# Convolution results stored as 196 pixels a quarter in column order, centering products over four rounds, raw weights two rounds later

## The chip, the cores and the metric

The kernel runs on one core of one Trainium2 chip, in float32 throughout. The metric is the time of the program on the device, in microseconds (us). The kernel before took 2997.26 us, the median of 3 runs (2994.66 to 2997.37).

TensorE (PE) multiplies matrices and writes its results to PSUM, an accumulation memory of eight banks. VectorE (DVE) and ScalarE (ACT) work elementwise on PSUM and on SBUF, the on-chip memory; GpSimd (POOL) works on SBUF. SyncE (SP) and ScalarE issue the transfers, which 16 DMA engines carry out.

## The reference

The input x is 32 images of 384 channels and 28 x 28 pixels. A ConvNeXt block with a response normalisation is followed by a gate over channels:

```python
y = conv_general_dilated(x, dw_w, (1, 1), [(3, 3), (3, 3)], feature_group_count=C) + dw_b
mu, var = mean(y, channels), mean(square(y - mu), channels)
y = (y - mu) * rsqrt(var + 1e-6) * ln_g + ln_b
y = gelu(y @ w1 + b1)                       # 384 -> 1536
gx = sqrt(sum(square(y), pixels))
y = grn_g * (y * gx / (mean(gx, features) + 1e-6)) + grn_b + y
x = x + y @ w2 + b2                         # 1536 -> 384
avg, mx, mn = mean(x, pixels), max(x, pixels), min(x, pixels)
logits = concat(avg @ W1.T, grouped(mx, W2_1) * W2_2, mn @ W3.T) @ Wfc.T
out = sigmoid(logits + x)
```

## The kernel before, in words

There are two stages.

**The convolution stage** runs 48 rounds (`NK`), of 8 channels each, over all 32 images at once. In a round, `conv` (L733) multiplies turned image rows (`xt`) with small banded matrices of the taps (`tmat`), 160 matmul instructions, into four PSUM tiles `pc`. `settle` empties them: ScalarE adds the bias and writes `ye` (L754), DVE adds the results into the running channel sum `acc` (L761), and DVE transposes blocks of 32 x 32, so that images come to lie on partitions (L767). The result `yt` holds, for each partition (a quarter of the rows of one image: 4 quarters x 32 images) and each of the 8 channels, 7 rows of 32 places, of which 28 are pixels and 4 are a gap: `YP` = 224 places for `YR` = 196 pixels. ScalarE squares the pixels (L778) and POOL adds the squares (L781). Two transfers on ScalarE's queue store `yt` to the DRAM tensor `yd` (L850). DVE also turns the image rows for the round after next (`turn_x`, L526). Two sets of four PSUM tiles alternate, so `conv` of a round waits until the round two before has been emptied.

SP loads in program order: image rows five rounds ahead (`load_x`, L466), tap tables (`load_t`, L485), and what the table `loads` sets for a round. Every instruction of this stage is held in program order on its engine. A transfer also waits, before its issue, on the signal that it takes over from a transfer about a dozen earlier.

Beside the convolution the weights are prepared. The first weight matrix is loaded in three parts (`raw1`) in rounds 5, 6 and 7. In round 9, behind the convolution's matmuls, `center_sums` does 72 matmul instructions (36 products of two instructions) with `ln_b` and `ln_g` (L640); DVE takes out the new bias and the column means `mcol`. In rounds 10, 11 and 12 `center_means` spreads the means over the partitions and `center_w` takes them out of the weights (L671). From round `U1` = 13 on, `form_w` makes the first layer's sums of weight blocks on POOL and ScalarE (L610 to L616), which SP stores to DRAM (L857) two rounds later. The second matrix is loaded by `raw2` from round `U2` - 3 on, and its 38 forms are made in rounds `U2` = 26 to `U2E` = 45.

**The image stage** runs over the 32 images; each has two products, done with fewer multiplications through sums of blocks. `load_y` loads an image's convolution results from `yd` into `yi` (L332), `normed` multiplies them by the inverse deviation `rb` (L352), POOL makes sums of rows of blocks (`forms_up`, L396), `up` does the first product (L982), ScalarE the gelu (L930) and the squares (L950), POOL sums of blocks again (`sums`, L1119), and `down` the second product (L1156) in 38 steps of 3 products. DVE adds each step's PSUM result `pz` to the quarters of the image `xt` that it belongs to (L1172; L1174 where it is the last term of a quarter, with the bias and a sum). Quarter j of an image is the rows 4k + j. `gate_store` computes the gate and stores the image. While one image goes down, gelu and squares of the next lie beside it on ScalarE; a planner sets the order of what isn't held.

Of the kernel before, what the change touches and what calls it, by code (L numbers as in the profile page):

```python
# [14 lines left out]
P = 128  # L15
C = 384
# [205 lines left out]
def convnext_gate_kernel(  # L222
# [18 lines left out]
    smp = ctx.enter_context(tc.tile_pool(name="smp", bufs=3))  # L241

    fs = [dram.tile([P + 1, FL], F32, name=f"fs_{cb}") for cb in range(CB)]
    yd = dram.tile([P, C, YP], F32, name="yd")
    rsd = dram.tile([P, YR], F32, name="rsd")
    u1d = dram.tile([KT, P, NS, P], F32, name="u1d")
    u2d = dram.tile([ND // UD, P, UD * KD * P], F32, name="u2d")
# [53 lines left out]
    EARLY_G = (0, 1)  # L301

    def load_y(b):
        yi = yis[b] = yip.tile([P, CB, NQD, YP], F32, tag="yi", name=f"yi_{b}")

        with tc.issue_after(last_u2[-1]) if last_u2 else ExitStack():
            for cb in range(CB):
                ins = load_y_part(b, yi, cb, 0, P)
                if b == 1:
                    tc.keep_in_program_order(ins)  # L310
        if b > 1:
            load_rb(b)
# [21 lines left out]
            yd.rearrange("(q b) c n -> b c q n", b=B)[b, cb * P + p0 : cb * P + p1],  # L334
        )

    def rows(v):

        return v.rearrange("p q (k w) -> p (q k) w", w=PW)[:, :, :HW]

    def flat(v):

        return v.rearrange("p q n -> p (q n)")

    def normed(b, cbs=range(CB)):

        if b not in accs:
            accs[b] = (
                xp.tile([P, CB, NT], F32, tag="x", name=f"acc_{b}") if b == 1 else room_acc
            )  # L350
        for cb in cbs:
            ins = nc.vector.tensor_tensor(  # L352
                accs[b][:, cb].rearrange("p (k w) -> p k w", w=HW),
                rows(yis[b][:, cb]),
                rbs[b].rearrange("p q (k w) -> p (q k) w", w=HW),
                ALU.mult,
            )
            if b <= 2:
                tc.keep_in_program_order(ins)
# [40 lines left out]
    with ExitStack() as one:  # L400
# [13 lines left out]
            return pscs[(n_now + other) % 2].tile([P, 512], F32, tag="pc", name=name)  # L414


        scr = yip.tile([P, CB, NQD, YP], F32, tag="yi", name="scr")
        scr = scr.rearrange("p k q n -> p (k q n)")
        nscr = 0

# [129 lines left out]
        w1r = ws.rearrange("p (k f) -> p k f", f=FF)  # L550
        w1v = ws.rearrange("p (k t m c) -> p t k m c", t=KT, m=3, c=P)
        w2v = ws.rearrange("p (t k m c) -> p t k m c", t=KD, k=4, c=P)
        U1, U2, U2E = 13, 26, NK - 3
        stores = []
        SG = 24

# [83 lines left out]
                nc.tensor.matmul(dst, w, v, start=False, stop=True, skip_group_check=True)  # L640
            )

        def center_sums(pb):

            for n in range(FB):
                for cb in range(CB):
                    end_product(
                        pb[:, 2 * n : 2 * n + 2], w1r[:, cb, n * P : (n + 1) * P], lr[:, cb]
                    )
# [55 lines left out]
        for n, f, *args in (  # L705
            (0, load_x, 2, (0, 1)), (0, load_x, 2, (1, 2)),
            (1, load_t, 1), (3, vectors),
            (2, load_x, 3, (0, 1)), (2, load_x, 3, (1, 2)),
            (3, load_x, 4, (0, 1)), (3, load_x, 4, (1, 2)),
            (13, gate_rows), (14, load, wfc[: 3 * R], wfcT), (15, load, w22b, w22.broadcast_to([P, R])),  # L710
            (4, load_t, 2), *((5 + i, raw1, i) for i in range(CB)),
            *((k - 5, load_x, k // XR, (k % XR, k % XR + 1)) for k in range(5 * XR, NK)),
            *(
                (TR * m - 6 + q, load_t, m, None, (q,))
                for m in range(3, NK // TR)
                for q in range(NQD)
            ),
            *((U2 - 3 + i, raw2, i) for i in range(3)),
        ):
            loads[n].append((f, args))  # L720
# [21 lines left out]
        def settle(n, pcs, yt):  # L742

            ye = yep.tile([P, NQD, 2, NN], F32, tag="ye", name=f"ye_{n}")
            last = n == NK - 1
            for q in range(NQD):
                for g in range(2):
                    c = TC * n + 2 * q + g
                    dst, src = ye[:, q, g, :], pcs[q][:, g * NN : (g + 1) * NN]
                    if last and q >= 2:  # L750
                        keep(nc.vector.tensor_scalar(dst, src, dwb[:, c : c + 1], None, ALU.add))
                    else:
                        keep(
                            nc.scalar.activation(  # L754
                                dst, src, AF.Identity, bias=dwb[:, c : c + 1], scale=1.0
                            )
                        )
            def sums():

                for q in range(NQD):  # L760
                    keep(nc.vector.tensor_tensor(acc, acc, pcs[q][:, : 2 * NN], ALU.add))  # L761

            if not last:
                sums()
            for h in range(2):
                keep(
                    nc.vector.transpose(  # L767
                        yt[:, 2 * h : 2 * h + 2].rearrange("p q g (k w) -> p (q g k) w", w=PW),
                        ye[:, 2 * h : 2 * h + 2].rearrange("p q g (k b) -> p (q g k) b", b=PW),
                    )  # L770
                )
            yv = yt.rearrange("p q g (k w) -> p (q g k) w", w=PW)[:, :, :HW]
            if last:
                sums()
            if n >= NK - 2:
                direct(n, yt)
            sq = sqp.tile([P, TC * YR], F32, tag="sq", name=f"sq_{n}")
            keep(nc.scalar.activation(sq.rearrange("p (k w) -> p k w", w=HW), yv, AF.Square))  # L778
            for h in range(2):
                keep(  # L780
                    nc.gpsimd.tensor_tensor(  # L781
                        ssum, ssum, sq[:, h * NQD * YR : (h + 1) * NQD * YR], ALU.add
                    )
                )

        def direct(n, yt):

            c0 = (TC * n) % P
            for h in range(NQD):
                keep(  # L790
                    (nc.scalar if n == NK - 1 else nc.sync).dma_start(
                        yis[0][c0 : c0 + TC, CB - 1, h, :],
                        yt[h * B : h * B + 1].rearrange("p q g n -> p (q g) n"),
                    )
                )

        def first_image(cb):

            keep(
                nc.scalar.activation(  # L800
                    room_acc[:, cb].rearrange("p (k w) -> p k w", w=HW), rows(yis[0][:, cb]),
                    AF.Identity,
                )
            )

        accs[0] = room_acc
        for n in range(NK):
# [12 lines left out]
            ends = [p[:, 2 * NN :] for p in pcs]  # L820
            if n == 6:
                end_product(ends[0][:, :NV], vrows, ident[:, :NV])
            if n == 9:
                center_sums(ends[0])
            if n == SG:
                for cb in range(CB):
                    end_product(
                        ends[cb][:, : 3 * R], wfc[:, cb * P : (cb + 1) * P],
                        ident[:, : 3 * R],
                    )  # L830
            if 10 <= n < 10 + CB:
                center_means(n - 10)
            yt = ycp.tile([P, NQD, 2, YP], F32, tag="yc", name=f"yt_{n}")
            if n + 2 < NK:
                turn_x(n + 2)
# [1 line left out]
            if n == 6:  # L837
                keep(nc.vector.tensor_copy(vecs, ends[0][:, :NV]))
                keep(nc.vector.tensor_copy(lr[:, :, 0], lnb_t))
                keep(nc.vector.tensor_scalar(lr[:, :, 1], lng_t, -1.0 / C, None, ALU.mult))  # L840
            if n == 9:
                pbv = ends[0][:, : 2 * FB].rearrange("p (f v) -> p f v", v=2)
                keep(nc.vector.tensor_tensor(b1f, pbv[:, :, 0], b1_t, ALU.add))
                keep(nc.vector.tensor_copy(mcol, pbv[:, :, 1]))
            if 10 <= n < 10 + CB:
                center_w(n - 10)
            for h in range(2):
                c0 = TC * n + NQD * h
                keep(
                    nc.scalar.dma_start(  # L850
                        yd[:, c0 : c0 + NQD, :],
                        yt[:, 2 * h : 2 * h + 2].rearrange("p q g n -> p (q g) n"),
                    )
                )
            while stores and stores[0][0] <= n:
# [2 lines left out]
            if 2 <= n < CB + 1:  # L858
                sequences(n - 1)
            if n == NK - 11:  # L860
                yis[0] = yip.tile([P, CB, NQD, YP], F32, tag="yi", name="yi_0")
# [146 lines left out]
    def finish(part):  # L1008
# [3 lines left out]
        if part == 1:  # L1012
# [7 lines left out]
            )  # L1020
            keep(
                nc.vector.tensor_scalar(
                    mu.rearrange("p (k w) -> p k w", w=HW),
                    turned.rearrange("p (k w) -> p k w", w=PW)[:, :, :HW],
                    dws, 1.0 / C, ALU.add, ALU.mult,
                )
# [49 lines left out]
    def sums(b):  # L1076

        if b not in ops:
# [7 lines left out]
            if b >= max(1, B - 2):  # L1086


                n = KD * NQ4
                if b == B - 2:  # L1090
                    more = yip.tile([P, CB, NQD, YP], F32, tag="yi", name="more")
# [40 lines left out]
    def down(b, hooks):  # L1132
# [13 lines left out]
        for i, (opnd, _, bk, reads) in enumerate(STEPS):  # L1146
# [244 lines left out]
```

## Time and profile before

| what | value |
|---|---|
| median of 3 runs | 2997.26 us |
| the profiled execution's own time | 2999.83 us |
| its span, first to last instruction | 2998.1 us |
| PE busy | 2924.5 us (98%) |
| DVE busy | 2014.6 us (67%) |
| ACT busy | 1761.2 us (59%) |
| POOL busy | 2365.0 us (79%) |
| DMA moved | 614.51 MB, mean 205 GB/s |
| store yd<-yt | 96 of 448 KB, 5.1 us to landing |
| load yi<-yd | 95 of 448 KB, 6.0 us to landing |

In the profile, L12 is line 12 of the kernel; `yt<-ye` means that the tile yt is written from ye. The page's forty slices show each engine's busy share in tenths, TensorE's granted clock and the DMA engines' share. A group's row has the count, the busy time, the mean of one instruction in ns, and the idle time of its engine just before, with what ended it. The chain is followed back from the last instruction, at each step to what released it. A busy PE is not PE at its peak, since matmuls are pipelined.

### The profile page before, as it was taken

The numbers are of one execution on the slowest core, as the hardware profiler recorded it, in microseconds if no ns is written. First come the engines' busy times: TensorE is split into PE (matmuls) and PEld (weight loads), VectorE is DVE, ScalarE is ACT, GpSimd is POOL, SyncE is SP. The second block draws the span as 40 slices with busy tenths as digits, with TensorE's granted clock in tenths as the row PEclk, the third lists the DMA queues.
The fourth block names the chain that finished last, engine by engine and source line by source line (L and its number), as shares of the span: only waits on it lengthen the run. The fifth ranks groups of instructions, "written<-read, shape, count | busy, mean of one in ns | idle before, by whom it ended". The sixth has DMA issues, their size and how long they took to land.

```text
span 2998.1 us, 53084 instructions
## 1 busy us (share of the span) xinstructions
PE 2924.5 (98%) x19156; PEld 2304.5 (77%) x19156; DVE 2014.6 (67%) x4444; ACT 1761.2 (59%) x2854; POOL 2365.0 (79%) x1768
## 2 busy tenths in 40 slices
PE   9998998899999999999999999999999999999998
PEld 8777774777777777777777777777777777777777
DVE  5677777766666666666666666666666666666665
ACT  3454565656666666666666666556666666666671
POOL 2356657888888888888888888888888888888897
PEclk9898999999999999999999999999999999999999
DMA  9789966556666666666666666666666656666545
GB/s 249 215 258 279 289 229 203 175 179 191 195 193 200 200 202 201 200 198 197 199 201 205 206 204 209 201 203 206 205 201 187 208 190 190 193 198 200 196 149 197
DMA packets 281263, 614.51 MB, mean 205 GB/s; under 512 B 26587, under 2 KB 102057, under 8 KB 281001
## 3 DMA queue, kind: packets, MB, share of 16 engines
q1 hardware_dynamic: 253154, 526.62, 57.0%
q10 hardware_dynamic: 27846, 84.49, 7.6%
q8 instruction: 154, 2.52, 0.4%
q14 instruction: 109, 0.88, 0.1%
HBM read 516.47 MB, written 94.48 MB: 204 GB/s over the span
## 4 chain that ended last, share of the span: by engine, by line
PE 83%; DMA 6%; DVE 4%; POOL 3%; issue 2%; ACT 1%; SPq 0%; ACTq 0%; DVEq 0%; POOLq 0%
PE ph_C L982 14%; PE ph_A L982 13%; PE ph_B L982 12%; PE pz_A L1156 8%; PE pz_C L1156 8%; PE pz_D L1156 7%; PE pz_F L1156 7%; PE pc L733 4%; PE pz_H L1156 2%; PE pz_I L1156 2%; PE pz_E L1156 2%; DMA yd<-yt 2%; DVE room L352 1%; PE pz_B L1156 1%; PE pz_G L1156 1%
## 5 line engine op out<-in xcount | busy, mean ns | idle before, releaser
L365 ACT ACTIVATE y<-y,vecs,gsc 128x784 f32<-128x784 f32 x375 | 359.9, 1030 | 446.3 <-DVE gsc L1064 446.3
L1119 POOL TENSOR_TENSOR d_room<-y 128x588 f32<-128x588 f32 x250 | 359.8, 1443 | 293.9 <-PE pz_B L1156 217.8
L930 ACT ACTIVATE y<-y,b1f 128x784 f32<-128x784 f32 x384 | 348.0, 945 | 221.4 <-DVE y L1001 197.3
L982 PE MATMUL ph_C<-room,ws 128*128 128x392 f32 x1224 | 456.4, 494 | 3.7 <-DVE y L999 2.4
L982 PE MATMUL ph_A<-room,ws 128*128 128x392 f32 x1220 | 454.1, 494 | 5.0 <-ACT te L991 5.0
L1119 POOL TENSOR_TENSOR d_room<-d_room,y 128x588 f32<-128x588 f32 x308 | 442.8, 1442 | 16.7
L982 PE MATMUL ph_B<-room,ws 128*128 128x392 f32 x1220 | 452.2, 493 | 1.4 <-DVE te L999 1.4
L733 PE MATMUL pc<-xt,tmat 28*128 28x224 f32 (+3 forms) x7680 | 383.7, 362 | 33.8 <-DVE stats L761 17.0
L733 PEld LDWEIGHTS pc<-xt,tmat 28*128 28x128 f32 (+2 forms) x7680 | 318.3, 173 | 97.3 <-issue 45.1
L982 PEld LDWEIGHTS ph_C<-room,ws 128*128 128x128 f32 x1224 | 230.6, 190 | 181.8 <-DVE y L999 21.3
L982 PEld LDWEIGHTS ph_A<-room,ws 128*128 128x128 f32 x1220 | 232.2, 190 | 175.5 <-ACT te L991 5.6
L982 PEld LDWEIGHTS ph_B<-room,ws 128*128 128x128 f32 x1220 | 231.7, 191 | 164.2 <-DVE te L999 2.2
L781 POOL TENSOR_TENSOR stats<-stats,sq 128x784 f32<-128x784 f32 x96 | 177.6, 1850 | 223.6 <-ACT sq L778 219.8
L950 ACT ACTIVATE stats<-y 128x784 f32<-128x784 f32 x381 | 326.8, 858 | 9.0
L1119 POOL TENSOR_TENSOR d_room<-y,d_room 128x588 f32<-128x588 f32 x214 | 306.6, 1439 | 27.0 <-PE pz_D L1156 15.9
L396 POOL TENSOR_TENSOR room<-room 128x392 f32<-128x392 f32 x298 | 298.8, 1019 | 11.6
L1119 POOL TENSOR_TENSOR y<-y 128x588 f32<-128x588 f32 x180 | 258.5, 1436 | 6.5
L997 DVE TENSOR_TENSOR y<-y,ph_B 128x392 f32<-128x392 f32 x252 | 135.5, 558 | 151.4 <-ACT y L930 123.5
L995 DVE TENSOR_TENSOR y<-y,ph_C 128x392 f32<-128x392 f32 x386 | 216.3, 562 | 27.4 <-ACT y L991 0.9
L1156 PE MATMUL pz_A<-d_room,u 128*128 128x196 f32 x1050 | 204.7, 330 | 1.8 <-DMA u<-u2d 0.8
L761 DVE TENSOR_TENSOR stats<-stats,pc 128x448 f32<-128x448 f32 x192 | 119.1, 620 | 114.8 <-ACT ye L754 96.1
L1156 PEld LDWEIGHTS pz_A<-d_room,u 128*128 128x128 f32 x1050 | 178.2, 190 | 10.8 <-POOL d_room L1119 1.8
(277 smaller groups left out, 5495.7 us busy)
## 6 DMA issues: line engine op xcount, KB each, us to landing
u<-u2d SPq DMA_DIRECT2D x487, 384.0 KB, 3.8
ws<-u1d SPq DMA_DIRECT2D x380, 320.0 KB, 3.0
ws<-u2d SPq DMA_DIRECT2D x121, 384.0 KB, 4.1
yd<-yt ACTq DMA_DIRECT2D x96, 448.0 KB, 5.1
yi<-yd SPq DMA_DIRECT2D x95, 448.0 KB, 6.0
x<-in_x SPq DMA_DIRECT2D x32, 1176.0 KB, 5.6
out<-x ACTq DMA_DIRECT2D x31, 1176.0 KB, 7.6
xi<-in_x SPq DMA_DIRECT2D x120, 196.0 KB, 6.0
```

What stands on the lines that cost most here:

```text
L365: eng.activation(out, in_, AF.Identity, bias=add, scale=mul)
L396: tc.keep_in_program_order(eng.tensor_tensor(d, o[in0], o[in1], op))
L733: nc.tensor.matmul(pcs[q][PW * j0 : PW * j1, g * NN + k0 * PW : g * NN + k1 * PW], t[PW * q : PW * q + HW, m0 : m0 + PW * (j1 - j0)], xt[P ...
L761: keep(nc.vector.tensor_tensor(acc, acc, pcs[q][:, : 2 * NN], ALU.add))
L781: nc.gpsimd.tensor_tensor(ssum, ssum, sq[:, h * NQD * YR : (h + 1) * NQD * YR], ALU.add)
L930: ins = nc.scalar.activation(y, y, AF.Gelu, bias=b1f[:, f : f + 1], scale=1.0)
L950: ins = nc.scalar.activation(stats[:, :NT], ys[b][:, f, :], AF.Square, accum_out=ssqs[b][:, f : f + 1])
L982: ins = nc.tensor.matmul(banks[t, bk][:, :NH], wts[t, g][:, gi, :], o[opnd], start=(first == 1), stop=True, skip_group_check=True,)
L995: ins = nc.vector.tensor_tensor(d, d, p, ALU.add)
L997: ins = nc.vector.tensor_tensor(d, d, p, ALU.subtract)
L1119: eng.tensor_tensor(d[0], o[a][0], o[c][0], ALU.add if sign == "+" else ALU.subtract)
L1156: nc.tensor.matmul(pz[:, :NQ4], wt[:, i % UD, t, :], o[opnd][0][:, t, :], start=(first and t == 0), stop=(t == KD - 1), skip_group_check=True,
```

## The change

The results between the stages lose their gaps. The transpose now writes each block so that pixels lie in column order: place w * 7 + k for column w and row k of a quarter, so that the 196 pixels come first and the 28 places of the four gap columns last. `yd` and `yi` hold 196 places a quarter, and the two stores a round leave the gap out. Everything between works on 196 pixels in column order; `normed` and `first_image` read without gaps. Where column order meets row order again, the pattern of one operand changes: the channel mean `mu` in `finish` is written in column order, and in `down` the PSUM result is read in steps of 7 places, against rows of the image.

The 36 centering products of round 9 are spread over rounds 10 to 13, nine in each; the means and `center_w` move from rounds 10 to 12 to rounds 12 to 14. The three loads of the first matrix move from rounds 5 to 7 to rounds 7 to 9. `U1` goes from 13 to 15 and `U2` from 26 to 28, with all that hangs on them (the forms, their stores, the three loads of the second matrix), while the end `U2E` stays.

```diff
-    yd = dram.tile([P, C, YP], F32, name="yd")
+    yd = dram.tile([P, C, YR], F32, name="yd")
...
-        yi = yis[b] = yip.tile([P, CB, NQD, YP], F32, tag="yi", name=f"yi_{b}")
+        yi = yis[b] = yip.tile([P, CB, NQD, YR], F32, tag="yi", name=f"yi_{b}")
...
             ins = nc.vector.tensor_tensor(
-                accs[b][:, cb].rearrange("p (k w) -> p k w", w=HW),
-                rows(yis[b][:, cb]),
-                rbs[b].rearrange("p q (k w) -> p (q k) w", w=HW),
+                accs[b][:, cb], flat(yis[b][:, cb]), flat(rbs[b]),
                 ALU.mult,
             )
...
-        U1, U2, U2E = 13, 26, NK - 3
+        U1, U2, U2E = 15, 28, NK - 3
...
-        def center_sums(pb):
+        NC, FC = 10, 3
 
-            for n in range(FB):
+        def center_sums(g, pb):
+
+            for n in range(g * FC, (g + 1) * FC):
                 for cb in range(CB):
                     end_product(
...
-            (4, load_t, 2), *((5 + i, raw1, i) for i in range(CB)),
+            (4, load_t, 2), *((7 + i, raw1, i) for i in range(CB)),
...
                     nc.vector.transpose(
-                        yt[:, 2 * h : 2 * h + 2].rearrange("p q g (k w) -> p (q g k) w", w=PW),
-                        ye[:, 2 * h : 2 * h + 2].rearrange("p q g (k b) -> p (q g k) b", b=PW),
+                        yt[:, 2 * h : 2 * h + 2].rearrange("p q g (w k) -> p (q g) k w", w=PW),
+                        ye[:, 2 * h : 2 * h + 2].rearrange("p q g (k b) -> p (q g) k b", b=PW),
                     )
...
-            yv = yt.rearrange("p q g (k w) -> p (q g k) w", w=PW)[:, :, :HW]
+            yv = yt.rearrange("p q g n -> p (q g) n")[:, :, :YR]
...
-            if n == 9:
-                center_sums(ends[0])
+            if NC <= n < NC + FB // FC:
+                center_sums(n - NC, ends[0])
...
-            if 10 <= n < 10 + CB:
-                center_means(n - 10)
+            if NC + 2 <= n < NC + 2 + CB:
+                center_means(n - NC - 2)
...
-            if n == 9:
-                pbv = ends[0][:, : 2 * FB].rearrange("p (f v) -> p f v", v=2)
-                keep(nc.vector.tensor_tensor(b1f, pbv[:, :, 0], b1_t, ALU.add))
-                keep(nc.vector.tensor_copy(mcol, pbv[:, :, 1]))
-            if 10 <= n < 10 + CB:
-                center_w(n - 10)
+            if NC <= n < NC + FB // FC:
+                fs_now = slice((n - NC) * FC, (n - NC + 1) * FC)
+                pbv = ends[0][:, : 2 * FB].rearrange("p (f v) -> p f v", v=2)[:, fs_now]
+                keep(nc.vector.tensor_copy(mcol[:, fs_now], pbv[:, :, 1]))
+                keep(
+                    nc.vector.tensor_tensor(b1f[:, fs_now], pbv[:, :, 0], b1_t[:, fs_now], ALU.add)
+                )
+            if NC + 2 <= n < NC + 2 + CB:
+                center_w(n - NC - 2)
...
                         yd[:, c0 : c0 + NQD, :],
-                        yt[:, 2 * h : 2 * h + 2].rearrange("p q g n -> p (q g) n"),
+                        yt[:, 2 * h : 2 * h + 2].rearrange("p q g n -> p (q g) n")[:, :, :YR],
...
-                    mu.rearrange("p (k w) -> p k w", w=HW),
+                    mu.rearrange("p (w k) -> p k w", w=HW),
...
-                pzh = pz[:, :NQ4].rearrange("p (k w) -> p k w", w=HW)
+                pzh = pz[:, :NQ4].rearrange("p (w k) -> p k w", w=HW)
```

More of the change, by code (lines that the diff above doesn't have):

```diff
@@ L335, in load_y_part @@
         )
-    def rows(v):
-        return v.rearrange("p q (k w) -> p (q k) w", w=PW)[:, :, :HW]
     def flat(v):
@@ L414, in bank1 @@
             return pscs[(n_now + other) % 2].tile([P, 512], F32, tag="pc", name=name)
-        scr = yip.tile([P, CB, NQD, YP], F32, tag="yi", name="scr")
+        scr = yip.tile([P, CB, NQD, YR], F32, tag="yi", name="scr")
         scr = scr.rearrange("p k q n -> p (k q n)")
@@ L777, in settle @@
             sq = sqp.tile([P, TC * YR], F32, tag="sq", name=f"sq_{n}")
-            keep(nc.scalar.activation(sq.rearrange("p (k w) -> p k w", w=HW), yv, AF.Square))
+            keep(nc.scalar.activation(sq.rearrange("p (c n) -> p c n", n=YR), yv, AF.Square))
             for h in range(2):
@@ L792, in direct @@
                         yis[0][c0 : c0 + TC, CB - 1, h, :],
-                        yt[h * B : h * B + 1].rearrange("p q g n -> p (q g) n"),
+                        yt[h * B : h * B + 1].rearrange("p q g n -> p (q g) n")[:, :, :YR],
                     )
@@ L800, in first_image @@
                 nc.scalar.activation(
-                    room_acc[:, cb].rearrange("p (k w) -> p k w", w=HW), rows(yis[0][:, cb]),
-                    AF.Identity,
+                    room_acc[:, cb], flat(yis[0][:, cb]), AF.Identity,
                 )
@@ L860, in convnext_gate_kernel @@
             if n == NK - 11:
-                yis[0] = yip.tile([P, CB, NQD, YP], F32, tag="yi", name="yi_0")
+                yis[0] = yip.tile([P, CB, NQD, YR], F32, tag="yi", name="yi_0")
             for cb in range(CB):
@@ L1090, in sums @@
                 if b == B - 2:
-                    more = yip.tile([P, CB, NQD, YP], F32, tag="yi", name="more")
+                    more = yip.tile([P, CB, NQD, YR], F32, tag="yi", name="more")
                     more = more.rearrange("p k q n -> p (k q n)")
```

## The prediction

> **What bounds the kernel now.** I read the page first, its busy shares and its forty slices.
>
> ```profile
> PE 2924.5 (98%) x19156; PEld 2304.5 (77%) x19156; DVE 2014.6 (67%) x4444; ACT 1761.2 (59%) x2854; POOL 2365.0 (79%) x1768
> PE   9998998899999999999999999999999999999998
> PEclk9898999999999999999999999999999999999999
> DMA  9789966556666666666666666666666656666545
> ```
>
> There are two stages. From slice 9 on (about 600 us) TensorE is full, at full clock, with DMA at 0.6. The waits of TensorE between 600 and 2850 us are only these:
>
> ```profile
> PE ph_C L982 <- DVE y L999: 2.4, 11, 0.5
> PE pz_A L1156 <- DMA u<-u2d: 0.8, 2, 0.4
> PE pz_A L1156 <- DVE x L1172: 0.7, 1, 0.7
> ```
>
> So nothing in that stage can become faster by a cheaper load or a cheaper DVE instruction: it can only become slower. The first 460 us, the convolution's 48 rounds, are different. In one window over them DMA stands at 0.85, TensorE at a granted clock of 0.89, DVE at 321.9 of 460 us. Undisturbed, 160 matmuls of a round take 7.2 us (the chain has 633 of them in 28.52 us); the 48 rounds take about 9 us each. All that this change can win lies here. The chain, in order of time, shows the one long piece that the change touches:
>
> ```profile
> 94.40 14.68 PE pc L733 x313
> 109.08 12.77 PE pc L640 x72
> 121.86 5.74 PE pc L733 x77
> ```
>
> and the stretches around it (columns: window, length, busy of PE, PEld, DVE, ACT, POOL, granted clock, DMA share, GB/s):
>
> ```profile
> 102.00:122.00 20.00, 20.00 (x268) 18.87 (x255) 7.95 (x10) 5.48 (x11) 7.38 (x4) 0.75 0.98 258
> 122.00:131.00 9.00, 9.00 (x168) 7.88 (x168) 6.64 (x10) 4.29 (x9) 1.65 (x1) 0.80 0.25 93
> 131.00:139.00 8.00, 7.90 (x169) 6.70 (x168) 6.15 (x9) 4.82 (x10) 2.04 (x2) 1.00 0.13 52
> ```
>
> While TensorE does the 72 centering products the transfers run ahead until their buffers are full, and then the DMA engines idle: 9.0 x 0.75 + 8.0 x 0.87 = 13.7 us of it.
>
> **Part 1: centering products spread, raw matrix later.** The work stays: 72 products x 178 ns = 12.8 us, now four times 3.2 us in rounds 10 to 13, and the eight mean products of three rounds (1.16 us each) two rounds later. The small DVE reads (0.13 and 0.15 us) become four pairs, +0.8 us in all on a DVE that has about 2 us a round free. What can be won is the idle DMA time: at most 13.7 us. The other bound is TensorE itself. Round 9 ends at 109.1; then four rounds of 7.2 + 3.2 us and two mean products give 153 us for the start of round 14, which now starts at 159.4. That is -6.5. With the rounds a little faster than 7.2 (the undisturbed ones of this stretch take 6.4) it is -9. I take **-8 us**. The three raw loads (768 KB each, SP queue) move from rounds 5 to 7 to rounds 7 to 9, past the image loads (four a round) and the tap-table loads of those rounds. DMA is full from 50 to 122 us, so the same bytes stall TensorE two rounds later; this I count as nothing. The cover is that round 10 needs the last one only at its end, some 10 us after its issue; were it late, the matmuls behind the centering products in TensorE's queue would wait, a few us. The second raw load, the forms and their stores move by two rounds, and 38 second-layer forms go into 17 rounds for 19. That is 12% more per round on POOL, which was busy 37.7 of 50 us at its fullest; some 2 us more in 50 fit. SP already waits 63.2 us for POOL before form stores, with image loads queued behind; I put 0 to +4 us on it and take 0, as nearly all of those waits are for forms that are stored two or three rounds after they are made.
>
> **Part 2: the packets.** A store of 448 KB in 128 packets of 3584 B becomes 392 KB in 512 packets of 784 B, since the 112 B gap now stands between quarters in SBUF. Two narrow windows price this. The first has only the two stores of one round (256 packets and 32 signals, 9 ns each by the packet records) in 4 us; the second, 3 us long, only the store of the row of statistics, 128 packets of 784 B from SBUF to DRAM, the very form that comes.
>
> ```profile
> q10 hardware_dynamic: 288, 0.92, 58.0%
> ```
> ```profile
> q1 hardware_dynamic: 144, 0.10, 10.5%
> ```
>
> 58.0% x 16 x 4 us is 37.1 us, less 0.3 for signals: 144 ns a packet. 10.5% x 16 x 3 us is 5.04 us, less 0.14: 38 ns a packet. A round's stores go from 256 x 144 = 36.9 to 1024 x 38 = 38.9 us of engine time: the 12.5% fewer bytes are eaten by the packets. Over 16 engines that is +0.12 us a round, +6 us if all 48 were bound by DMA; about 0.6 of the stage has DMA over 0.9, so **+3.6 us**. The bounds are -9 (bytes count, packets do not) and +6. The loads of it had 512 packets before (896 B); they get 7% shorter, in a stage where they are hidden.
>
> **Part 3: strides.** The transpose writes every 28 B in SBUF, and the additions of the second half read PSUM every 28 B. No row of this trace has such a stride. The nearest rows are the same instructions without it:
>
> ```profile
> L767 DVE STREAM_TRANSPOSE yt<-ye 128x896 f32<-128x896 f32 x96 | 100.7, 1087 | 1.6 <-ACT ye L754 1.6
> L1172 DVE TENSOR_TENSOR x<-x,pz_C 128x196 f32<-128x196 f32 x320 | 103.1, 355 | 78.8 <-PE pz_C L1156 78.5
> ```
>
> An element costs 1.04 ns (392 elements 558 ns, 196 elements 355). Two rules of the Trainium skill part here. "VectorE: DVE Perf Modes", section on mode 1x, says that fp32 with odd strides still makes one result a cycle: +0. "SBUF — State Buffer", section on the DMA port swizzle, says that SBUF is read in lines of 16 B and PSUM in lines of 8 B, that at least two hits a line hide the latency, and that each access to a new line pays. 28 B hit a new line every time; it gives no figure, so as an estimate from the rows I take a second cycle for each element: +0.93 us a transpose (96 of them) and +0.20 us an addition (51 an image). By the first rule parts 2 and 3 come to +3.6; by the second to +25 in each place, worked out under the rivals. I take the first, since 1.04 ns is one step of the engine and contiguous PSUM reads show no finer one, but keep the second in the range. The multiply at L352 loses its gaps (969 ns median); it lies behind a full TensorE, 0.
>
> **Sum.** 2999.8 us (the profiled execution; span 2998.1) - 8 + 3.6 = 2995.4. That execution stands 2.6 above the median 2997.3, so against the median **2993 us**, own range 2984 to 2999.
>
> **Rivals.**
> *Strided PSUM reads cost* (ends slower). The place is the end of each image's second half:
>
> ```profile
> 1528.00:1532.00 4.00, 4.00 (x26) 4.00 (x25) 2.83 (x9) 3.49 (x4) 2.22 (x3) 1.00 1.03 376
> 1532.00:1536.00 4.00, 4.00 (x15) 2.50 (x14) 3.97 (x10) 2.25 (x5) 3.84 (x4) 1.00 1.03 414
> ```
>
> (The third busy column is DVE.) DVE is at 2.83 and then 3.97 of 4 us, with reductions of 0.96 us behind the additions. Some 20 of an image's 51 additions fall in the last 14 us; 20 x 0.20 = 4 us against about 3 us of free time makes DVE some 1 us late where the next image's first results want their banks and DVE. 31 images x 0.8 us: **+25, 3018 us**. Earlier a step of TensorE is 0.99 us with at most two additions at a pitch of 0.27 us; at 0.47 they still fit. It decides from about +0.15 us an addition; at +0.3 (pitch 0.57 x 51 plus 10 us of other DVE work against 38 steps of 0.99 us) the whole half is bound by DVE, over 3035 us. For it: the 8 B line. Against: DVE sits idle before nearly every addition.
> *Strided SBUF writes cost.* A round of DVE takes 2.1 (turning images) + 2.9 (sums) + 2.1 (transposes) = 7.1 us; +1.9 makes 9.0, as long as the mean round. The rounds shorter than that would stretch by up to 1.9 us, some half of 48, less what DMA stalls hide: +25, **3018 us**.
> *The stores land later.* Each ring now holds 32 packets of a store for 8, in turn with 6 KB image packets of the SP queue. The stores' landing is 8.6% of the chain of the first 600 us, 52 us, and ScalarE waits at its store issue with the next round's eviction behind it, then DVE's sums, then TensorE two rounds on. A third longer: +17, less the gain of 8: **3006 us**. Against: image packets then pass the stores sooner, and those are on the chain as well.
> *Nothing changes*: the idle DMA time only moves to another round: **2997 us**.
>
> **How the numbers follow.** Chances: the forecast 0.40, PSUM reads 0.19, SBUF writes 0.13, later stores 0.15, nothing 0.13. A measurement here tells about 0.2%, 6 us, from no change. Of the forecast's 0.40, some 0.26 lies below 2991 and 0.13 within; with the few gains of "nothing" faster is 0.30. Within: 0.13 plus most of "nothing" plus a little of the later stores, 0.24. Slower 0.46, from the three costs. The range goes from 2984 to 3032: below lies 0.07, above (dear PSUM reads, or both strides) 0.11.
>
> **What would show it.** The group at L640 in four pieces of 3.2 us and DMA over 0.7 in the two rounds after round 9; L767 at 1087 and L1172 at 355 ns as before (right) or near 2000 and 560 (rivals one and two); queue 10 with 49,152 packets of 784 B at 38 ns; start of round 14 near 151 us. It is wrong if TensorE's waits in the second stage grow beyond 10 us, or if store landings pass 7 us.

## The result, and the profile after

The changed kernel takes **3041.6 us** (median, 3038.2 to 3043.0) against 2997.3 us (2994.7 to 2997.4): a ratio of **1.0136, 95% interval 1.0121 to 1.0151**. It is 44 us slower by these medians and 41 us by the ratio, which is used from here on; the forecast was 2993 us, with a range up to 3032.

The lines of the changed kernel's page that answer to the busy shares and slices of before:

```profile
PE 2941.0 (97%) x19156; PEld 2313.3 (76%) x19156; DVE 2082.3 (69%) x4450; ACT 1760.5 (58%) x2854; POOL 2366.2 (78%) x1768
...
PE   9987898899999999999999999999999999999998
...
PEclk9888888999999999999999999999999999999999
DMA  9879976545665666666665666656655565665545
```

DVE has 68 us more work, and TensorE's granted clock reads 8 (0.8 to 0.9) in slices 2 to 7, where before it read 8 in slices 2 and 4 alone. From slice 8 on TensorE's rows are the same as before. By the start times in the two traces:

| | before | after | difference |
|---|---|---|---|
| profiled span | 2998.1 | 3036.4 | +38.3 |
| start of round 14 | 159.4 | 154.8 | -4.6 |
| start of round 26 | 266.2 | 274.7 | +8.5 |
| end of the convolution (last matmul of `conv`) | 450.2 | 485.3 | +35.1 |
| third load of `rb` to the end (the image stage) | 2438.4 | 2439.0 | +0.6 |

So nearly the whole loss arises in the convolution stage, behind the start of round 14. The groups of the two strided instructions after the change (busy, mean ns, idle before):

```profile
L763 DVE STREAM_TRANSPOSE yt<-ye 128x896 f32<-128x896 f32 x96 | 164.8, 1795 | 1.7 <-ACT ye L750 1.7
L1170 DVE TENSOR_TENSOR x<-x,pz_C 128x196 f32<-128x196 f32 x320 | 103.1, 355 | 77.0 <-PE pz_C L1154 76.5
```

The transpose that writes SBUF every 28 B went from 1087 to 1795 ns. The addition that reads PSUM every 28 B takes 355 ns as before (the prediction shows both rows of before). `normed` (now L348) keeps its median of 968 ns (969 before). Stores and loads between the stages, first the queue's line before and then the changed kernel's lines (packets, MB, share of 16 engines; below it KB and median us to landing):

```profile
q10 hardware_dynamic: 27846, 84.49, 7.6%
```
```profile
q10 hardware_dynamic: 64710, 78.98, 8.3%
...
yd<-yt ACTq DMA_DIRECT2D x96, 392.0 KB, 6.9
yi<-yd SPq DMA_DIRECT2D x95, 392.0 KB, 5.5
```

Fewer bytes take more engine time. By the packet records of the convolution stage's stores alone it is 142.6 us of each engine for 119.3: 49,184 packets of 784 B at 46.4 ns for 12,288 of 3584 B at 155 ns.

The centering products, in the chain of waits in order of time (start, length), and the windows where the DMA engines idled before, with the next 16 us:

```profile
114.16 6.10 PE pc L729 x113
120.25 2.10 PE pc L634 x18
122.35 7.96 PE pc L729 x160
130.31 2.10 PE pc L634 x18
```
```profile
122.00:131.00 9.00, 9.00 (x171) 8.01 (x170) 8.27 (x11) 4.73 (x10) 3.70 (x2) 0.81 0.88 199
131.00:139.00 8.00, 8.00 (x130) 7.75 (x137) 6.55 (x8) 3.62 (x9) 3.69 (x2) 0.79 1.03 251
139.00:155.00 16.00, 16.00 (x273) 13.95 (x258) 11.83 (x18) 6.38 (x12) 5.38 (x3) 0.89 0.63 162
```

A piece of 18 product instructions takes 2.1 us, and DMA stands at 0.88 and 1.03 where it stood at 0.25 and 0.13. Part of the idle time has moved behind it: 0.63 from 139 to 155 us, for 0.79 before.

**A loop that the prediction did not look at.** The timelines of a calm stretch of each kernel (start, length, engine, count; in brackets the wait ahead of it), first before, then after:

```profile
167.90 2.80 ACT L754 ACTIVATE ye<-pc,dwb 128x224 f32<-128x224 f32 x8
168.70 2.89 DVE L761 TENSOR_TENSOR stats<-stats,pc 128x448 f32<-128x448 f32 x4 [1.39 <-ACT ye L754]
171.50 2.10 DVE L767 STREAM_TRANSPOSE yt<-ye 128x896 f32<-128x896 f32 x2
173.70 1.51 ACT L778 ACTIVATE sq<-yt 128x1568 f32<-128x1568 f32 x1 [3.00 <-DVE yt L767]
...
175.63 2.80 ACT L754 ACTIVATE ye<-pc,dwb 128x224 f32<-128x224 f32 x8
```
```profile
307.70 2.80 ACT L750 ACTIVATE ye<-pc,dwb 128x224 f32<-128x224 f32 x8
...
308.50 2.89 DVE L757 TENSOR_TENSOR stats<-stats,pc 128x448 f32<-128x448 f32 x4 [0.43 <-ACT ye L750]
311.31 3.47 DVE L763 STREAM_TRANSPOSE yt<-ye 128x896 f32<-128x896 f32 x2
314.89 1.51 ACT L774 ACTIVATE sq<-yt 128x1568 f32<-128x1568 f32 x1 [4.39 <-DVE yt L763]
...
316.72 2.80 ACT L750 ACTIVATE ye<-pc,dwb 128x224 f32<-128x224 f32 x8
```

Each step begins when the one above it ends or is under way: ScalarE evicts, DVE sums, DVE transposes, ScalarE squares, and only then, because the square stands ahead of it in ScalarE's program order, comes the next round's eviction. (A weight form's copy of 0.5 to 0.6 us, among the lines left out, lies between square and eviction as well.) One turn takes 7.73 us before and 9.02 us after, +1.29, where the pair of transposes grew by 1.37. ScalarE waits 3 to 4.4 us for the transposes in each turn. DVE, with 2.1 us for turning images besides, has 7.05 us of work in the turn of 7.73: it is nearly full too, so that the timeline alone does not tell the loop from DVE's busy time. By the starts of the evictions of rounds 2 to 45 the shortest turn was 7.2 us before and 8.5 after. An eviction began on the mean 6.0 us after the round's convolution had ended, and 7.4 us in the changed kernel, so it was not TensorE, nor its lower clock, that held it up.

### The profile page after: what moved, and what is told of

Read it like the earlier page. It is cut to its first block, busy times and chain, and to the rows that moved or that the text cites. A ratio compares the mean times of both kernels' runs of the same rounds, so it can differ in the third digit from the quotient of the medians.

```text
span 3036.4 us, 53090 instructions
## 1 busy us (share of the span) xinstructions
PE 2941.0 (97%) x19156; PEld 2313.3 (76%) x19156; DVE 2082.3 (69%) x4450; ACT 1760.5 (58%) x2854; POOL 2366.2 (78%) x1768
## 4 chain that ended last, share of the span: by engine, by line
PE 81%; DMA 7%; DVE 5%; POOL 2%; issue 2%; ACT 1%; SPq 0%; ACTq 0%; DVEq 0%; POOLq 0%
PE ph_C L980 14%; PE ph_A L980 13%; PE ph_B L980 12%; PE pz_A L1154 8%; PE pz_C L1154 8%; PE pz_D L1154 7%; PE pz_F L1154 7%; PE pc L729 3%; DMA yd<-yt 2%; PE pz_H L1154 2%; PE pz_I L1154 2%; PE pz_E L1154 2%; DVE yt L763 2%; DVE room L348 1%; DMA u<-u2d 1%
## 5 line engine op out<-in xcount | busy, mean ns | idle before, releaser
L729 PE MATMUL pc<-xt,tmat 28*128 28x224 f32 (+3 forms) x7680 | 405.1, 369 | 51.3 <-DVE stats L757 30.2
L729 PEld LDWEIGHTS pc<-xt,tmat 28*128 28x128 f32 (+2 forms) x7680 | 332.7, 177 | 121.5 <-DVE stats L757 60.2
L774 ACT ACTIVATE sq<-yt 128x1568 f32<-128x1568 f32 x48 | 72.6, 1512 | 216.7 <-DVE yt L763 180.4
```

Source lines behind the costliest of these rows:

```text
L729: nc.tensor.matmul(pcs[q][PW * j0 : PW * j1, g * NN + k0 * PW : g * NN + k1 * PW], t[PW * q : PW * q + HW, m0 : m0 + PW * (j1 - j0)], xt[P ...
L774: keep(nc.scalar.activation(sq.rearrange("p (c n) -> p c n", n=YR), yv, AF.Square))
```

## The experiments

Two theories. **The loop**: eviction, sums, transposes, square, next eviction is a serial chain that sets the pace of the rounds, so that time added to it counts though both engines have free time. **Busy time**: DVE's and the DMA engines' sums of work set the pace, and the order on ScalarE does not matter. Besides, the parts of the change had to be separated. Kernels are compared by their ratios to the kernel before, measured beside them on the same chip (0.001 is 3 us; a ratio is known to about 0.0008 to 0.0016, so the difference of two kernels to some 3 to 7 us).

### The change taken apart: four kernels

**e1**, the kernel before with the moved steps alone:

```diff
-        U1, U2, U2E = 13, 26, NK - 3
+        U1, U2, U2E = 15, 28, NK - 3
...
-            (4, load_t, 2), *((5 + i, raw1, i) for i in range(CB)),
+            (4, load_t, 2), *((7 + i, raw1, i) for i in range(CB)),
...
-            if n == 9:
-                center_sums(ends[0])
+            if NC <= n < NC + FB // FC:
+                center_sums(n - NC, ends[0])
```

> The kernel before with the centering products, the raw loads and the form rounds moved, and nothing else. Both theories (strided transpose writes, small store packets) hold the loss in the layout: they expect a gain here, of 8 us by the prediction, 4.6 us by where round 14 starts in the changed kernel: 2989 to 2993 us, with 72 centering matmuls in four pieces. If the moved steps were what costs, 3005 us or more.

**e2**, the changed kernel with a transpose that writes without a stride:

```diff
-                        yt[:, 2 * h : 2 * h + 2].rearrange("p q g (w k) -> p (q g) k w", w=PW),
+                        yt[:, 2 * h : 2 * h + 2].rearrange("p q g (k w) -> p (q g) k w", w=PW),
```

> The changed kernel with the transpose writing rows again, in one run of 896 places, so that the stores take the first 196 of 224 places in row order and pixels land in wrong places; packets, schedule and image stage as in the changed kernel. Stride theory: the transpose is back at 1087 ns, the convolution stage ends near 450 us, 2993 to 3000 us. Packet theory: transpose 1087 ns but the time stays at 3030 to 3040 us, landing of the stores near 7 us.

**e3**, the changed kernel that stores and loads whole quarters of 224 places:

```diff
-    yd = dram.tile([P, C, YR], F32, name="yd")
+    yd = dram.tile([P, C, YP], F32, name="yd")
...
-                        yt[:, 2 * h : 2 * h + 2].rearrange("p q g n -> p (q g) n")[:, :, :YR],
+                        yt[:, 2 * h : 2 * h + 2].rearrange("p q g n -> p (q g) n"),
```

> The changed kernel with whole quarters of 224 places stored and loaded (128 packets of 3584 B a store), the gap at the end of each quarter; the transpose still writes every 28 B. Stride theory: transpose 1796 ns, stage end near 485 us, 3035 to 3042 us. Packet theory: stores land in 5.1 us again, 2993 to 3000 us. A mixture shows as something between, and says how much each is worth.

**e4**, the changed kernel with the steps moved back (the diff of e1 turned round):

> The changed kernel with the centering products, raw loads and form rounds put back; the layout alone. Both theories: the loss without the gain of the moved steps, 3045 to 3050 us. If the moved steps gain nothing once DVE is the slowest: 3041 us as the changed kernel. If they were what costs: near 3000 us.

| kernel | moved steps | stride | 784 B packets | us | ratio (95%) | convolution ends | transpose ns | stores, us of each engine |
|---|---|---|---|---|---|---|---|---|
| e1 | yes | no | no | 2993.6 | 0.9975 (0.9966-0.9984) | 445.7 | 1086 | 119.0 |
| e2 | yes | no | yes | 3008.2 | 1.0019 (1.0012-1.0027) | 453.2 | 1086 | 144.6 |
| e3 | yes | yes | no | 3025.7 | 1.0077 (1.0063-1.0090) | 477.3 | 1792 | 121.2 |
| e4 | no | yes | yes | 3045.0 | 1.0145 (1.0128-1.0161) | 487.1 | 1793 | 142.6 |
| changed | yes | yes | yes | 3041.6 | 1.0136 (1.0121-1.0151) | 485.3 | 1795 | 142.6 |

The moved steps alone: -7.5 us. The packets (e2 less e1): +13 us, and +18 by the changed kernel less e3. The stride (e3 less e1): +31 us, and +35 by the changed kernel less e2. Both e2 and e3 lie between what the two theories expected of them: each of the two parts costs, the stride more. The sum of the three is +36.5 and the whole +41, a gap that is within the uncertainty. With the layout in place the moved steps bring 3 us (changed less e4) with an uncertainty of 7, so whether they lose some of their gain there can't be told.

The stride's price is not paid in every round. From e1 to e3 the pair of transposes grew by 1.34 us (from the first one's start to the second one's end), 64 us over 48 rounds, and the time by 31. By the eviction starts of rounds 2 to 45 the shortest turn grew from 7.2 to 8.4 us, nearly the full price, and the mean turn from 9.16 to 9.80, about half of it.

### What a stride costs, and where

**e5**, the kernel before with six strides in turn, one a round: of the two transposes one writes, the other reads, in steps of 1, 2, 4, 7, 14 and 28 places, and the sums read PSUM and write `acc` in the same steps. It ran once, and only the durations of its instructions are read.

```diff
+            def steps(t, h, s):
+                return t[:, h * M : (h + 1) * M].rearrange("p (a w s) -> p a s w", s=s, w=PW)
...
+                    pv = lambda s: pcs[q][:, :N2].rearrange("p (w s) -> p s w", s=s)
+                    av = lambda s: acc.rearrange("p (s w) -> p s w", s=s)
```

> The kernel before, with the pattern of the transposes and of the channel sums changed from round to round: in round n, the first transpose writes, the second reads, and the four sums read PSUM, in steps of 1, 2, 4, 7, 14 or 28 places of 4 B, by n mod 6, the other side of each being contiguous. Pixels and channel sums land in wrong places; the work is the same. Each step has its own line. A cost of the 16 B line in SBUF: 1087 ns up to a step of 2 (two places a line), 1790 at 7 and above, a step of 4 (one place a line) as 7. A cost that grows with the step: 14 and 28 above 1800. Reads as writes, if the line is what counts. PSUM: 620 ns at each step, as the additions of the image stage show at 7; with an 8 B line that costs, 2 and above slower.

Groups by line and form of e5: write steps of 2, 4 and 28 places (L800, L803, L812), read steps of 2, 4 and 28 (L801, L804, L813), and sums in steps of 1 and 28 (L766, L776):

```profile
L800 DVE STREAM_TRANSPOSE yt<-ye 128x896 f32<-128x896 f32 x8 | 8.8, 1106 | 0.0
L803 DVE STREAM_TRANSPOSE yt<-ye 128x896 f32<-128x896 f32 x8 | 14.3, 1790 | 0.0
L812 DVE STREAM_TRANSPOSE yt<-ye 128x896 f32<-128x896 f32 x8 | 14.6, 1821 | 1.6 <-ACT ye L754 1.6
L801 DVE STREAM_TRANSPOSE yt<-ye 128x896 f32<-128x896 f32 x8 | 8.6, 1070 | 0.0
L804 DVE STREAM_TRANSPOSE yt<-ye 128x896 f32<-128x896 f32 x8 | 13.8, 1720 | 0.0
L813 DVE STREAM_TRANSPOSE yt<-ye 128x896 f32<-128x896 f32 x8 | 14.0, 1746 | 0.0
...
L766 DVE TENSOR_TENSOR stats<-stats,pc 128x448 f32<-128x448 f32 x32 | 19.8, 619 | 16.2 <-ACT ye L754 13.1
L776 DVE TENSOR_TENSOR stats<-stats,pc 128x448 f32<-128x448 f32 x32 | 19.8, 620 | 16.4 <-ACT ye L754 13.5
```

A transpose pays a flat 0.6 to 0.7 us as soon as its steps are 4 places (16 B), for reads as for writes; at 2 places (8 B) it pays nothing. At 7 and 14 places it took 1807 and 1717 ns written, 1730 and 1645 read. A sum of two operands pays nothing at any step, in PSUM or in SBUF. So the stride costs this instruction and not the addition; why it does is not shown.

### The loop or the busy time

**e6**, e1 with a transpose of 512 places into a spare tile ahead of each of the round's two; it lengthens DVE's work about as the stride does, without a stride:

```diff
             for h in range(2):
+                keep(
+                    nc.vector.transpose(
+                        pad.rearrange("p (k w) -> p k w", w=PW),
+                        ye.rearrange("p q g n -> p (q g n)")[:, : 16 * PW].rearrange(
+                            "p (k b) -> p k b", b=PW
+                        ),
+                    )
+                )
                 keep(
                     nc.vector.transpose(
```

> The kernel before with the moved steps of e1, and ahead of each transpose a second one of 512 contiguous places into a tile that nobody reads, some 0.63 us of DVE, as much as the strided write added; no stride anywhere. If DVE's time alone is what the stride costs: as far above e1 as e3 was, 31 us, near 3024 us. If the strided write hurts in another way too (other engines' or the transfers' access to SBUF): clearly less, under 3012 us.

3024.0 us, 1.0074 (1.0059 to 1.0090): +30 us over e1, as e3 has. The added pair makes the round's transposes 1.19 us longer, for the stride's 1.34. So the time that DVE spends there explains the stride's cost to within the 5 us of the comparison; nothing else of the stride is needed. The row of the added transposes:

```profile
L770 DVE STREAM_TRANSPOSE pad<-ye 128x512 f32<-128x512 f32 x96 | 66.0, 687 | 1.3 <-ACT ye L757 1.3
```

**e10**, e6 with the two added transposes behind the round's own (their arguments cut here):

```diff
             for h in range(2):
-                keep(nc.vector.transpose(pad..., ye...))
                 keep(nc.vector.transpose(yt..., ye...))
+            for h in range(2):
+                keep(nc.vector.transpose(pad..., ye...))
```

> The kernel of e6 with its two added transposes of 512 places (some 0.63 us each by their pitch) behind the round's own transposes instead of ahead of them: the same DVE work, but the square on ScalarE need not wait for it. If the loop ScalarE - DVE - ScalarE sets the pace, most of e6's 30 us over e1 goes: 2995 to 3010 us. If it is DVE's busy time that counts, it stays at e6's 3020 to 3028 us.

3004.0 us, 1.0005 (0.9999 to 1.0012): +9 us over e1. DVE's added work is no smaller here (the four transposes take 1.34 us more than the two of e1), yet it costs 30 us where the square waits for it and 9 where it does not. About two thirds are the loop, a third is DVE's busy time or what else is behind it.

**e9**, e1 with ScalarE's square and the two stores of a round issued after the next round's eviction:

```diff
+            held_yt[n] = yt
+            for m in sorted(held_yt):
+                if m < n or n >= NK - 3:
+                    put(m, held_yt.pop(m))
```

(`put` holds the square, the sums of squares on POOL and the two stores, all as they were.)

> The kernel of e1 (moved steps alone, old layout) in which ScalarE's squares and the two stores of a round are issued after the next round's eviction instead of before it; nothing is added or removed. If the serial loop eviction - sums - transposes - square - next eviction on ScalarE and DVE sets the pace of the convolution stage, the square leaves the loop, the stage falls toward what DVE's work alone (7.1 us a round) or the DMA engines allow: 20 to 60 us below e1, 2940 to 2975 us, and ScalarE's waits of sq for the transposes nearly vanish. If DVE's busy time or DMA bounds the stage, the order on ScalarE makes no difference: 2988 to 2997 us, as e1.

**2960.3 us, 0.9866 (0.9851 to 0.9881)**: 33 us below e1 and 40 below the kernel before, with no work removed. The convolution ends at 412.8 us. ScalarE's wait of the square for the transposes in the first 490 us, in e1 and then in e9 (total, times, longest):

```profile
ACT sq L780 <- DVE yt L769: 125.8, 40, 6.9
```
```profile
ACT sq L783 <- DVE yt L769: 8.1, 3, 5.0
```

A busy-time bound would have left the time as it was. In this kernel DVE is busy 281 of the 350 us from 50 to 400, for 253 in e1, and DMA stands at 0.90 in both. The eviction waits for the convolution more often instead (30.1 us in 14 rounds of the first 440 us, before the change 13.4 in 3). This is a version that beats both kernels. The square and the stores were moved together; which of them matters more was not separated.

**e12**, the changed kernel with the same deferral:

> The changed kernel with the deferral of e9: squares and stores of a round after the next round's eviction. If the loop sets the pace, the deferral gains at least as much here as in e9, since the loop is 1.4 us longer: 40 to 80 us below the changed kernel, 2960 to 3000 us, and what is left over e9 is the packets' 10 to 15 us and whatever of the stride shows where DVE's 8.4 us a round bind. If DVE's busy time sets it, 3035 to 3043 us as before.

2995.6 us, 0.9981 (0.9973 to 0.9989): 46 us below the changed kernel. The deferral brings more here than in e9, as the loop was longer. Stride and packets now cost 34 us (e12 less e9), for 48 without it (changed less e1 by the ratios). That they still cost as much is no longer the loop alone: DVE is busy 312 of 350 us and DMA stands at 0.97. How the 34 us divide between the two was not tried.

**e8**, e1 with the gaps taken out by a copy on ScalarE, ahead of the square, and the stores in packets of 3136 B; the copy's target needs room, so `yt` has one buffer for three:

```diff
+            keep(
+                nc.scalar.activation(
+                    yz.rearrange("p c (k w) -> p (c k) w", w=HW), yv, AF.Identity
+                )
+            )
```

> e1 with the gaps taken out by a copy on ScalarE (1.5 us a round, into a tile without gaps, in row order), the squares reading that tile, and stores of 128 packets of 3136 B; the transpose contiguous, the image stage in row order without gaps. Engine time of the stores falls by an eighth (119 to some 105 us over 16 engines), ScalarE gains 72 us of work that it has room for, but the stores go out 1.5 us later. If transfers set the pace: 2 to 8 us under e1, 2986 to 2992 us. If ScalarE's chain from transpose to store sets it: 5 to 20 us above e1.

3030.0 us, 1.0093 (1.0075 to 1.0110): +35 us over e1, more than either expectation, though the stores' engine time falls to 105.3 us, DMA from 0.90 to 0.82 (50 to 400 us), and ScalarE in e1 was busy only 175 of these 350 us. The copy puts 1.5 us into the loop, 72 us over 48 rounds, and about half of it is paid, as with the stride. DVE has as much work as in e1 (2021 us in the whole run for 2018). The single `yt` shows as no wait: by the trace the transposes waited once, 3.1 us, and for the eviction. So work on the other engine of the loop costs as much as work on DVE.

### Packets and the raw matrix

**e11**, e2 with each 784 B packet cut into two of 392 B:

```diff
-                        yd[:, c0 : c0 + NQD, :],
-                        yt[:, 2 * h : 2 * h + 2].rearrange("p q g n -> p (q g) n")[:, :, :YR],
+                        yd[:, c0 : c0 + NQD, :].rearrange("p c (u m) -> p (c u) m", u=2),
+                        yt[:, 2 * h : 2 * h + 2].rearrange(
+                            "p q g (u m) -> p (q g u) m", u=2
+                        )[:, :, : YR // 2],
```

> The kernel of e2 (contiguous transposes) whose stores go out in 1024 packets of 392 B for 512 of 784 B, the same bytes (98 of each 112 places; so pixels lie in wrong places, as in e2). If the number of packets is what e2 pays for over e1, this doubles it: 2048 packets a round at 25 to 35 ns are 51 to 72 us of engine time for 48, +0.2 to +1.5 us a round, 3012 to 3040 us, with landings past 8 us. If e2's cost has another cause, such as the loads' 784 B, it stays at 3004 to 3012 us.

3092.0 us, 1.0303 (1.0287 to 1.0319), 85 us over e2 and far above either expectation. The number of packets counts, as expected, and the price was wrong: the small packet takes 45.3 ns, nearly as much as the 784 B one (47.0 in e2), not 25 to 35. The stores then take 278.5 us of each engine, and the DMA share reads 1.10 from 50 to 400 us. Set against e1: +25.6 us of engine time cost e2 13 us (0.52 of it), +159.5 cost e11 98 us (0.62 of it). So the cost of packets goes with their engine time, near the share of 0.6 that the prediction took. It goes with the stores' landing too, 5.5 us in e1; no run parts the two. The stores in e2 and then in e11:

```profile
yd<-yt ACTq DMA_DIRECT2D x96, 392.0 KB, 7.7
```
```profile
yd<-yt ACTq DMA_DIRECT2D x96, 392.0 KB, 10.4
```

**e7**, e1 with the raw matrix loaded in rounds 5 to 7 as before:

```diff
-            (4, load_t, 2), *((7 + i, raw1, i) for i in range(CB)),
+            (4, load_t, 2), *((5 + i, raw1, i) for i in range(CB)),
```

> e1 with the raw loads back in rounds 5 to 7; the centering products stay spread over rounds 10 to 13 and the forms stay two rounds later. If the gain of e1 is that TensorE no longer holds 12.8 us at once: the same gain, 2992 to 2996 us. If the later loads are what gains: 3000 us or more.

2997.2 us, 0.9981 (0.9974 to 0.9989), 5.7 us under the kernel before by the ratio. The later loads are worth 0.0006, which the two intervals can't tell from nothing. The gain of e1 lies in the spreading, together with the later forms, from which no run parts it.

## Why the prediction was wrong

Two terms of the sum failed. Part 3 put the strided transposes at +0, and they cost 31 to 35 us; part 2 put the packets at +3.6, and they cost 13 to 18. Behind the first stands a picture of the stage in which DVE had time to spare.

**What bounds the kernel.** Right that all of it would be decided before 460 us: the image stage moved by 0.6 us. Wrong in what sets the pace there. The prediction named DMA and "the other bound is TensorE itself", read the rounds of 9 us against TensorE's 7.2, and gave DVE "about 2 us a round free". DVE did have some free time, but ahead of its sums, where it waited for the eviction; behind the transposes the square and the next eviction waited for it. Work added there was paid for, about half of its sum over the rounds (e3, e6, e8). That wait was to be seen in the profile of before: ScalarE waited 138.6 us for the transposes in 44 rounds.

```profile
ACT sq L778 <- DVE yt L767: 138.6, 44, 7.5
```

**Part 1, centering products.** Forecast -8 us, measured -7.5 alone. The start of round 14 was put near 151 us; it is 149.4 in e1, 154.8 in the changed kernel, where the slower rounds already count. That the number fits is in part luck: the pieces were put at 3.2 us and take 2.1 to 2.9 in e1, while the convolutions of rounds 11 to 13 take 8.3 to 8.8 us for the 7.2 assumed, and of the 10 us won at round 14 some 4.5 are left at the end of the convolution (450.2 to 445.7). Counting the later raw loads at nothing was right within what can be told (e7); the later forms were not tried alone.

**Part 2, packets.** Forecast +3.6 us, measured +13 (+18 with the stride in place). That the packets' engine time counts, at a share near 0.6, fits e2 and e11; the term that was too small is the price of a packet. 38 ns was read in a window in which the engines were about a tenth busy; between the image loads the same packet takes 47.0 ns, 24% more, while the long packet went from 144 to 155 ns, 8%. With the engine time of these two prices the sum is +25.6 x 0.6 = +15. The rival "stores land later" is not refuted: it had the landings right (5.1 to 6.9 us, a third longer; 7.7 in e2), and its +17 us is near e2's +13. The lower bound of -9 us is not on the footing of the upper one, +6: with all 48 rounds counted it is -14; nothing hangs on it.

**Part 3, strides.** The choice between the two rules of the Trainium skill was wrong for the transpose and right for the additions. "VectorE: DVE Perf Modes", section on mode 1x, gave +0, and the transpose took +0.71 us. The line of 16 B in "SBUF — State Buffer", section on the DMA port swizzle, agrees with where the transpose's cost sets in (none at 8 B, all of it at 16 B); the estimate of a second cycle, +0.93, was a third too high. For the additions neither line had an effect, the measurement against the page: 355 ns at 28 B in PSUM, and 619 to 621 ns at every step up to 112 B in PSUM and SBUF (e5). The sentence that failed is "1.04 ns is one step of the engine and contiguous PSUM reads show no finer one": it argued from additions about a transpose, of which no row had a stride.

**The rivals.** "Strided SBUF writes cost", held at 0.13 and +25 us, is what happened: +31 to +35. That it comes so close is in part luck. Half of the rounds is what was paid, but its 1.9 us a round were 1.3 to 1.4, and the deduction for DMA stalls, from some 46 us to 25, was not there: 1.34 x 24 is 32. Its reason was DVE's 9.0 us of work against the mean round; by e10 DVE's busy time explains at most about a third of such a cost. "Strided PSUM reads", with the larger chance, did not happen. TensorE's waits in the image stage, as far as the trace's list goes, are some 12 us from 600 to 2850 us for 4 before, past the 10 named as a sign, yet the stage is no longer for it (+0.6 us). The largest:

```profile
PE ph_C L980 <- DVE y L997: 5.3, 18, 0.7
PE pz_E L1154 <- POOL y L1117: 2.1, 1, 2.1
PE pz_H L1154 <- POOL d_room L1117: 1.7, 1, 1.7
```

With the measured terms in place of the forecast's, 2997.3 - 7.5 + 13 + 31 comes to 3034 us; by the ratio the changed kernel stands at 3038, and the gap is within the uncertainty.

## What to carry to other kernels

When no engine of a stage is full, look for a loop across engines: follow one round from an instruction to its next occurrence in the timeline, and see which instruction stands ahead of it only by program order. Work added to that loop costs time even on an engine with free time (here about half of it, on DVE as on ScalarE), and moving instructions behind the next round's first (here the square and the stores) can be worth more than the edits around it: 33 us of 2994. Price a changed packet in a window with the traffic that it will meet, and a changed stride by a row of the same instruction, or keep its upper price in the forecast.

## What the hardware showed that was not expected

- A fp32 transpose on DVE of 128 x 896 places takes 1070 to 1106 ns contiguous or in steps of 8 B, and 1645 to 1821 ns in steps of 16 to 112 B, whether the read or the write has the step (steps between 8 and 16 B were not tried). An addition of two operands of 448 places takes 619 to 621 ns at all of these, with PSUM and SBUF in the same step.
- A stored packet of 392 B took nearly as much time of a DMA engine as one of 784 B, 45.3 (e11) and 47.0 ns (e2), in a stage with other traffic.
